# Softmax sums of layer 1: exponentials of two of four key tiles added by accumulating DMAs

## The chip, the cores and the metric

The kernel runs on one core of a Trainium2 chip. The metric is the time of the whole program on the device in microseconds (us), one launch, the median of several runs. The core has TensorE (PE: matrix products from SBUF into PSUM), VectorE (DVE), ScalarE (ACT), GpSimd (POOL) and SyncE (SP). Each works through its own queue of instructions in order, and semaphores tie the queues together. DMA engines, shared by all queues, move data between HBM and SBUF and inside SBUF.

## The reference

Input x is 8 sequences of 512 tokens and 256 channels, with a context of 512 x 128 for each. Layer 0 has self and cross attention and a quantized MLP; layer 1 has two attention blocks, each with an MLP behind it, and a feed-forward part with a convolution. The change lies in the attention of layer 1. It has 16 heads of width 32; `x` is the query side, and `y` is `x` itself in the first block ("a1") and the context in the second ("a2"):

```python
q = jnp.einsum('bsc,hcd->bhsd', xn, wq)
k = jnp.einsum('btc,hcd->bhtd', yn, wk)
v = jnp.einsum('btc,hcd->bhtd', yn, wv)
a = jax.nn.softmax(jnp.einsum('bhsd,bhtd->bhst', q, k) * D ** (-0.5), axis=-1)
if causal:
    mask = (jnp.arange(t)[None, :] > jnp.arange(s)[:, None]).astype(a.dtype)
    a = a * mask
o = jnp.einsum('bhst,bhtd->bhsd', a, v)
```

The mask of the first block comes after the softmax: the sum below the fraction runs over all 512 keys, and only the product with V leaves keys out. So every exponential goes into the sum, and the masked ones alone into the product.

## The kernel before

Everything here is float32 except the quantized products. The attention of layer 1 is cut into 16 slots (8 sequences x 2 blocks); a slot has 4 groups of 4 heads, a group has 4 key tiles of 128 keys. Layer 1 thus has 64 groups and 256 steps. In the causal block (`blk` 0, "strict") the key tiles are taken from the last to the first; in the other from the first to the last. "Third" and "fourth" tile below means `n` = 2 and `n` = 3 of that order, counted from 0.

A step has two halves in `steps1` (L2191 on). `front(g, n)` makes on TensorE the scores of one key tile for 4 heads into two PSUM tiles `ps_s`, and on ScalarE the exponentials into `pt`, 128 keys x 4 heads x 512 queries, 1 MB; there are three buffers of `pt` (`PTS`). In the causal block GpSimd cuts the diagonal part of `pt` out into `dg` (L2221). `back(g, n)` multiplies with V into the PSUM bank `ov`, of which there is one; the four tiles of a group add up in it.

The sums of the softmax: VectorE adds the exponentials of the first three tiles into `acc` (L2246 for the first two, L2248 for the third), and after the last tile TensorE multiplies a column of ones with `acc` and with the fourth `pt` into a PSUM bank `sm`, so that each of a head's 32 output rows holds the sum. VectorE then transposes, takes the reciprocal, transposes back (L2261 to L2264) and multiplies: `oT` = `ov` x `rb` (L2266). That reads `ov` in PSUM, so the bank comes free only then. `oT` (five buffers) goes into the MLP, `mlp1`, which asks for `q["oT", blk, g]`.

What runs in which order is written at build time by a planner. `weave_all` (L1824) holds a list of the attention steps and several chains of streams: `first` (end of layer 0), `pair1` (Q and K of a group), `mlp1` for each half of a sequence, `pre1`, `values2`, `last` (final feed-forward part) and others. A stream is a generator that yields `need(...)`: the tiles it waits for. The planner keeps a clock for every engine (`Pace`) and takes, of what can start within 0.3 us, that with the lowest place in the order. So every engine's order is fixed before the program runs, and an instruction that comes later than planned holds back all that stands behind it on its engine. At most two fronts run ahead of the backs. `front_at` and `back_at` say when a half may start; the last back of a group waits for `acc` and for a PSUM bank.

For a DMA the planner has this rule (`Pace.note`):

```python
if ins.opcode == "DMACopy":
    self.free[e] = t0 + 0.4
    ...
    self.wire = max(self.wire, t0 + 1.2) + n / 280e3
    end = self.wire + 1.2
```

`t0` is when the issuing engine is free and the sources are ready; `n` is bytes, 280e3 stands for 280 GB/s. Who wrote the destination before does not count for a DMA.

GpSimd has three kinds of work in this part: the selects into `dg`, the reciprocal roots of the layer norms (`mv`, L1975 to L1978, two short instructions for each), and additions of rows to residuals (L2040, L2043, L2144, L2146). GpSimd issues no DMA in layer 1 after its first loads. SP issues all others.

Of the kernel before, what the change touches and what calls it, by code (L numbers as in the profile page):

```python
# [15 lines left out]
P = 128  # L16
# [935 lines left out]
class Fast(General):  # L952
# [814 lines left out]
    def layer1_xattn(self):  # L1767
        nc, tc = self.nc, self.tc
        with (
            tc.tile_pool(name="w2", bufs=1) as wpool,  # L1770
            tc.tile_pool(name="wst", bufs=1) as self.wst,
            tc.tile_pool(name="work2", bufs=1) as work,
            tc.tile_pool(name="small2", bufs=1) as self.small,
            tc.tile_pool(name="st1", bufs=2, space=PSUM) as self.st,
            tc.tile_pool(name="ac1", bufs=1, space=PSUM) as self.ovp,
            tc.tile_pool(name="m1a", bufs=3, space=PSUM) as self.m1,
        ):
            self.work = work
            self.seqs = {b: {} for b in range(B)}

            self.hps = [wpool.tile([P, T // 2 + 3], F32, name=f"hp{i}") for i in range(2)]
            for t in self.hps:
                nc.gpsimd.memset(t, 0.0)
            self.wl = {}


            self.pairs = self.fronts = self.backs = self.zTs = self.nvt = 0
            self.li1s, self.mlps, self.loads, self.both_in = [0, 0], [0, 0], {}, {}

            self.rows = [(blk, bs) for bs in ROWS for blk in range(2)]  # L1790
            order = self.order = [(b, blk) for blk, bs in self.rows for b in bs]
            few, pairs, mlps, pres = [], [], [[], []], [[], []]

            for k, b in zip(FIRST_AT, range(B)):
                few.append(Stream(self.first(b), 3.8, 0.8, k, 1.0))
                if b == 1:
                    few.append(Stream(self.load_mlp(), 1.0, 1.0, k))
            for k, b in zip(LAST_AT, range(B - 1)):
                few.append(Stream(self.last(b), 10.5, 0.8, k, 1.0))
            few.sort(key=lambda s: s.base)  # L1800
            for k, (b, blk) in enumerate(order):
                for half in range(2):
                    mlps[half].append(Stream(self.mlp1(b, blk, half), 20.5, 0.88 if blk else 0.5, k + 1))
                    if not blk:
                        pres[half].append(Stream(self.pre1(b, half), 7.5, 0.65, k - 1, 2.0))
                for g in range(4):
                    pairs.append(Stream(self.pair1(b, blk, g), 3.0, 0.2, k + 0.25 * (g - 1)))
            for half in range(2):
                mlps[half][-1].base += 0.4 * half
                mlps[half].append(Stream(self.tail(half), 20.0, 1.0, 17 + 0.4 * half))  # L1810
            vals = [Stream(self.values2(b), 1.0) for b, blk in order if blk]
            self.final, self.tails = {}, [0, 0]
            diag = [Stream(self.diagonals(), 1.0, 0.1, 15.5)]
            self.keys_done, self.x0_read = False, 0
            keys = [Stream(self.keys2_rest(), 8.0 * (B - KEYS_FIRST), 1.0, -1.0)]
            self.weave_all(
                [self.steps1(b, blk) for b, blk in order], [few, pairs, *mlps, *pres, vals, diag, keys]
            )
            self.pace.close()

# [3 lines left out]
    def weave_all(self, attns, chains):  # L1824

        pace = self.pace
        steps = [(k + n / len(a), 1.0 / len(a), s) for k, a in enumerate(attns) for n, s in enumerate(a)]
        chains = [list(c) for c in chains]  # L1830

        def advance(c):
            s, w = c[0], pace.work
            s.need = next(s.gen, None)
            s.done += pace.work - w
            if s.need is None:
                c.pop(0)

        def starts(s):
            names, on_pe, _, on = s.need  # L1840
            t = max(pace.when(names), pace.free[on] - s.lag)
            return max(t, pace.place("m1")) if on_pe else t

        while self.backs < len(steps) or any(chains):
            now = pace.free.get("PE", 0.0)
            cands = []
            for c in chains:
                while c:
                    s = c[0]
                    if s.need is WAIT:  # L1850
                        advance(c)
                        if c and c[0] is s and s.need is WAIT:
                            break
                    elif not s.need[1] and starts(s) <= now:
                        advance(c)
                    else:
                        cands.append((s.base + s.share * s.done / s.total, starts(s), lambda c=c: advance(c)))
                        break
            if self.fronts < len(steps) and self.fronts - self.backs < 2:
                at, _, s = steps[self.fronts]  # L1860
                cands.append((at, s[0](), s[2]))
            if self.backs < self.fronts:
                at, d, s = steps[self.backs]
                cands.append((at + 1.05 * d, s[1](), s[3]))
            can = [c for c in cands if c[1] <= now + 0.3]
            pick = min(can, key=lambda c: c[0]) if can else min(cands, key=lambda c: (c[1], c[0]))
            assert pick[1] < 1e8
            pick[2]()
# [322 lines left out]
    def steps1(self, b, blk):  # L2191
# [6 lines left out]
        slot = self.slot_of(b, blk)  # L2198
        st = {}

        def front_at(g):
            if ("QK", blk, g) not in q or ("vt", blk) not in q:
                return 1e9
            return max(pace.when([Pace.name(t) for t in q["QK", blk, g]]), pace.place("st", 2))

        def front(g, n):
            kt = order[n]
            self.fronts += 1
            QT, KT = q["QK", blk, g]
            diag = slice(kt * P, (kt + 1) * P)  # L2210
            pss = [self.st.tile([P, 2, T], F32, tag="st", name="ps_s") for _ in range(2)][::-1]
            for j in (2, 3, 0, 1):
                r = slice(32 * j, 32 * j + 32)
                self.mm(pss[j // 2][:, j % 2, :], KT[r, diag], QT[r, :])
            pt = work.tile([P, 4, T], F32, tag="pt", name="pt", bufs=PTS)
            for jp in (1, 0):
                nc.scalar.activation(pt[:, 2 * jp : 2 * jp + 2, :], pss[jp], AF.Exp)  # L2217
            parts = [(pt, slice(0, T))]
            if strict:
                dg = work.tile([P, 4, P], F32, tag="dg", name="dg", bufs=2)  # L2220
                nc.gpsimd.affine_select(  # L2221
                    out=dg, in_=pt[:, :, diag], compare_op=ALU.is_gt, fill=0.0,
                    base=0, pattern=[[0, 4], [-1, P]], channel_multiplier=1,
                )
                parts = [(pt, slice(0, kt * P))] if kt else []
                parts.append((dg, diag))
            st[g, n] = (kt, pt, parts)

        def back(g, n):
# [11 lines left out]
                        n == 0 and i == 0, n == NT - 1 and i == len(parts) - 1,  # L2241
                    )

            if n == 1:
                st["acc"] = work.tile([P, 4, T], F32, tag="acc", name="acc")
                nc.vector.tensor_tensor(st["acc"], st["pt"], pt, ALU.add)  # L2246
            elif n == 2:
                nc.vector.tensor_tensor(st["acc"], st["acc"], pt, ALU.add)  # L2248
            st["pt"] = pt
            if n < NT - 1:  # L2250
                return
            sm = self.bank()
            for k, t in enumerate((st["acc"], pt)):
                for j in (2, 3, 0, 1):
                    self.mm(sm[32 * j : 32 * j + 32, :], self.ones, t[:, j, :], k == 0, k == 1)

            if g == 0:
                st["recs"] = work.tile([P, 4, 16], F32, tag="recs", name="recs", bufs=2)
# [3 lines left out]
            nc.vector.reciprocal(rec, rt[:, :, 0])  # L2262
            rb = work.tile([P, T], F32, tag="rt", name="rb", bufs=1)
            nc.vector.transpose(rb, rec.unsqueeze(2).to_broadcast([P, 16, 32]))  # L2264
            oT = q["oT", blk, g] = work.tile([P, T], F32, tag="oT", name="oT", bufs=5)
            nc.vector.tensor_tensor(oT, ov, rb, ALU.mult)  # L2266
            if g == 3:
                self.seen(st["recs"])

        def back_at(g, n):  # L2270
# [2 lines left out]
                return 1e9  # L2273
            _, pt, parts = st[g, n]
            t = pace.when([Pace.name(pt), Pace.name(q["vt", blk])] + [Pace.name(p) for p, _ in parts])
            if n == 0:
                return max(t, pace.place("ov1"))
            return max(t, pace.when([Pace.name(st["acc"])]), pace.place("m1")) if n == NT - 1 else t

        return [  # L2280
            (lambda g=g: front_at(g), lambda g=g, n=n: back_at(g, n),
             lambda g=g, n=n: front(g, n), lambda g=g, n=n: back(g, n))
            for g in range(4) for n in range(NT)
        ]
# [317 lines left out]
```

## Time and profile before

| | |
|---|---|
| median of 3 runs | 2784.82 us (2781.45 to 2786.3) |
| span of the profiled execution | 2779.7 us |
| mean granted TensorE clock | 0.959 |
| stage of the 64 groups, first to last product with ones | 938.4 to 2612.8 us |
| exponentials of one tile, two instructions of 128x1024 | 1.02 us each |
| select of a diagonal part, alone | 0.63 us |
| transposes of the sums, each | 0.71 us |
| multiplication `ov` x `rb` | 0.69 us |
| copy of 128x512 from PSUM to SBUF | 0.69 us on VectorE, 0.585 us on ScalarE |
| DMA engines, mean busy share in the stage | 0.17 |

The profile is of one execution. Busy time is the time in which an engine worked; the rest it waited or had nothing to do. Matrix products in float32 are two records each, so 8 records are 4 products. Where a line names a releaser ("<- DVE oT L2266"), the engine stood idle until that instruction was done. "ps" is any PSUM bank of the shared pool, "ps_s" the scores, "ov" the bank of the V product. A DMA's time to landing runs from its issue until its semaphore is complete.

### The profile page before, as it was taken

Reading aid. Unit: us, or ns where it says so; the run is one execution under the profiler, and the core shown is the slowest. Engines: PE = TensorE matmul, PEld = TensorE weight load, DVE = VectorE, ACT = ScalarE, POOL = GpSimd, SP = SyncE. Lnnn points to the kernel's source line nnn. Section 1 sums busy time; section 2 is a strip of 40 time slices with the busy share of each in tenths; the row PEclk is TensorE's granted clock in tenths of the full one; section 3 lists DMA queues with packets and bytes.
Section 4 is the critical chain, followed back from the end, with each engine's and each line's share of the span. In section 5 each row is a group of like instructions: output and inputs, shape, how many; then the busy total and the mean of one; then the engine's idle time right before and its main releaser. Section 6 shows DMA issues by size and latency. Waiting matters only on the chain.

```text
span 2779.7 us, 38478 instructions
## 1 busy us (share of the span) xinstructions
PE 2517.8 (91%) x15447; PEld 1223.8 (44%) x15452; DVE 1736.5 (62%) x3135; ACT 1452.2 (52%) x1803; POOL 614.8 (22%) x682
## 2 busy tenths in 40 slices
PE   7999999999786989999999999988999989999875
PEld 2333333333233344535554535545455454454554
DVE  4544554343476666564666777676777877767766
ACT  4666666656573554445444455444554555555421
POOL 2212222111001344231334231111114332101100
PEclk9999999999886999999999999999999999999987
DMA  3001120000364512211211013211021102211010
GB/s 113 25 27 50 50 73 16 20 31 12 118 261 173 178 46 99 80 46 42 76 60 63 16 54 107 69 38 58 24 82 60 43 4 89 71 45 43 23 38 17
DMA packets 76475, 176.55 MB, mean 64 GB/s; under 512 B 7424, under 2 KB 36480, under 8 KB 68992
## 3 DMA queue, kind: packets, MB, share of 16 engines
q1 hardware_dynamic: 73904, 170.81, 17.6%
q8 instruction: 123, 2.02, 0.3%
q0 software_dynamic: 800, 2.62, 0.3%
q10 hardware_dynamic: 1584, 0.58, 0.1%
q14 instruction: 64, 0.52, 0.1%
HBM read 111.07 MB, written 62.91 MB: 63 GB/s over the span
## 4 chain that ended last, share of the span: by engine, by line
PE 46%; DVE 13%; ACT 4%; POOL 2%; issue 2%; DMA 0%; ACTq 0%; POOLq 0%; DVEq 0%; SPq 0%
PE ps L1053 31%; PE ps_s L1053 8%; PE ov L1053 6%; ACT pt L2217 2%; PE ps L1056 1%; DVE hF L2332 1%; DVE acc L2246 1%; POOL dg L2221 1%; DVE rb L2264 1%; DVE hm L2342 1%; DVE z L144 1%; DVE mv L1971 1%; DVE rt L2261 1%; DVE oT L2266 1%; DVE acc L2248 1%
## 5 line engine op out<-in xcount | busy, mean ns | idle before, releaser
L2217 ACT ACTIVATE pt<-ps_s 128x1024 f32<-128x1024 f32 x512 | 496.3, 1021 | 418.0 <-PE ps_s L1053 313.6
L1053 PE MATMUL ps_s<-QT,KT 32*128 32x512 f32 (+3 forms) x4096 | 613.2, 607 | 28.3 <-ACT pt L2217 16.1
L1431 ACT ACTIVATE pt<-ps_s 128x1024 f32<-128x1024 f32 (+3 forms) x512 | 411.2, 862 | 202.6 <-PE ps_s L1053 194.3
L1053 PEld LDWEIGHTS ps_s<-QT,KT 32*128 32x128 f32 x4096 | 191.6, 184 | 368.0 <-issue 201.8
L1053 PE MATMUL ps<-x3T,li 128*128 128x256 f32 x1024 | 244.9, 391 | 3.9 <-DVE hp L2320 2.4
L1053 PE MATMUL ov<-pt,v 128*32 128x512 f32 (+3 forms) x2048 | 232.7, 525 | 13.5 <-POOL pt L1434 12.7
L1053 PE MATMUL ps<-li,hD 128*128 128x256 f32 x1024 | 239.1, 389 | 5.7 <-ACT hD L2164 5.7
L1053 PE MATMUL ov<-pt,vt 128*32 128x512 f32 (+3 forms) x1792 | 204.4, 526 | 36.2 <-DVE oT L2266 29.4
L1977 POOL TENSOR_SCALAR mv<-mv 128x2 f32<-128x2 f32 (+1 forms) x105 | 57.7, 550 | 770.4 <-DVE mv L1972 735.3
L2221 POOL TENSOR_SCALAR_AFFINE_SELECT dg<-pt 128x512 f32<-128x512 f32 x128 | 116.1, 908 | 505.6 <-ACT pt L2217 505.4
L1053 PEld LDWEIGHTS ps<-x3T,li 128*128 128x128 f32 x1024 | 192.5, 194 | 60.7 <-issue 18.4
L1053 PEld LDWEIGHTS ps<-li,hD 128*128 128x128 f32 x1024 | 193.8, 194 | 56.4 <-issue 14.5
L1434 POOL TENSOR_SCALAR_AFFINE_SELECT pt<-pt 128x512 f32<-128x512 f32 x128 | 86.3, 674 | 471.7 <-ACT pt L1431 470.0
L2248 DVE TENSOR_TENSOR acc<-acc,pt 128x2048 f32<-128x2048 f32 x64 | 149.4, 2334 | 4.3 <-ACT pt L2217 3.2
L2246 DVE TENSOR_TENSOR acc<-pt 128x2048 f32<-128x2048 f32 x64 | 149.2, 2332 | 1.1 <-ACT pt L2217 1.1
L1456 DVE STREAM_TRANSPOSE ot<-ov 128x512 f32<-128x512 f32 x64 | 45.8, 716 | 165.9 <-PE ov L1053 165.9
L2332 DVE SCALAR_TENSOR_TENSOR hF<-hp,cols,hF 128x256 f32<-128x256 f32 x224 | 114.6, 512 | 41.7 <-ACT hF L2323 35.6
L1053 PE MATMUL ps<-zT,a_wq 128*128 128x512 f32 x256 | 127.8, 623 | 2.1 <-DVE zT L2058 2.1
L1053 PE MATMUL ps<-li,oT 128*128 128x256 f32 x512 | 128.0, 394 | 1.7 <-DVE oT L2266 1.0
L1759 ACT ACTIVATE hD<-ps,cols 128x256 f32<-128x256 f32 x123 | 54.7, 471 | 137.1 <-PE ps L1053 100.5
L1053 PEld LDWEIGHTS ov<-pt,v 128*32 128x32 f32 x2048 | 40.4, 108 | 167.1 <-issue 100.2
L1053 PEld LDWEIGHTS ps<-li,oT 128*128 128x128 f32 x512 | 92.9, 191 | 47.7 <-issue 16.1
(305 smaller groups left out, 3654.9 us busy)
## 6 DMA issues: line engine op xcount, KB each, us to landing
hd<-h SPq DMA_DIRECT2D x16, 1024.0 KB, 3.9
hF<-hd SPq DMA_DIRECT2D x16, 1024.0 KB, 6.7
li<-in_w_a_dram SPq DMA_DIRECT2D x12, 1024.0 KB, 5.0
fw<-q_f_w SPq DMA_DIRECT2D x22, 512.0 KB, 5.5
xF<-xd SPq DMA_DIRECT2D x22, 512.0 KB, 5.1
kd<-k SPq DMA_DIRECT2D x8, 1024.0 KB, 3.9
vd<-v SPq DMA_DIRECT2D x8, 1024.0 KB, 5.2
res<-rd SPq DMA_DIRECT2D x32, 256.0 KB, 2.8
```

The lines of the kernel that those rows point to most:

```text
L144: self.nc.vector.tensor_scalar(out[:, i, :], x[:, i, :], mv[:, i, 0:1], rstd[:, i : i + 1], ALU.subtract, ALU.mult,)
L1053: self.nc.tensor.matmul(out, lhsT, rhs, start=start, stop=stop, skip_group_check=True)
L1431: nc.scalar.activation(pt[:, 2 * jp : 2 * jp + 2, lo:], pss[jp][:, :, lo:], AF.Exp)
L1434: nc.gpsimd.affine_select(out=diag, in_=diag, compare_op=ALU.is_ge, fill=0.0, base=0, pattern=[[0, 4], [1, P]], channel_multiplier=-1,)
L1456: nc.vector.transpose(ot.rearrange("p b d -> p (b d)"), ov)
L1759: self.nc.scalar.activation(out, ps, AF.Identity, bias=bias)
L1977: nc.gpsimd.tensor_scalar(rstd, mv[:, :, 1], EPS, None, ALU.add)
L2217: nc.scalar.activation(pt[:, 2 * jp : 2 * jp + 2, :], pss[jp], AF.Exp)
L2221: nc.gpsimd.affine_select(out=dg, in_=pt[:, :, diag], compare_op=ALU.is_gt, fill=0.0, base=0, pattern=[[0, 4], [-1, P]], channel_multiplier=1,
L2246: nc.vector.tensor_tensor(st["acc"], st["pt"], pt, ALU.add)
L2248: nc.vector.tensor_tensor(st["acc"], st["acc"], pt, ALU.add)
L2332: nc.vector.scalar_tensor_tensor(a, hp[:, half + k : half + k + n], self.col("conv_w", 3 * f + k), a, ALU.mult, ALU.add)
```

## The change

In the attention of layer 1 the exponentials of the first two tiles are still added by VectorE, now in the front of the third tile. Those of the third and the fourth are added to `acc` by two DMAs that GpSimd issues, `accum_op=ALU.add`, each from `pt` to `acc`, 1 MB. The product with ones then has `acc` alone as its input, four products a group instead of eight.

The V product is copied out of its bank into `oT` straight after its last part (`copy_of`, ScalarE or VectorE, whichever the planner finds free first). The rest of the group becomes a stream of its own, `end`, which waits for `acc`, makes the sums, and multiplies `oT` in place. `weave_all` takes the list `self.ends` as a further chain; streams are added to it as groups finish, so chains are no longer copied. As there is one buffer of `acc`, the front of a third tile may start only when the sums of the group before have been issued (`self.summed`). `back_at` for the last tile no longer waits for `acc` or for a bank.

```diff
@@ layer1_xattn
+            self.ends, self.summed = [], 0
...
             self.weave_all(
-                [self.steps1(b, blk) for b, blk in order], [few, pairs, *mlps, *pres, vals, diag, keys]
+                [self.steps1(b, blk) for b, blk in order], [few, pairs, *mlps, *pres, vals, diag, keys, self.ends]
             )
@@ weave_all
-        chains = [list(c) for c in chains]
@@ steps1
-        def front_at(g):
-            if ("QK", blk, g) not in q or ("vt", blk) not in q:
+        def front_at(g, n):
+            if n == 2 and self.summed < 4 * slot + g or ("QK", blk, g) not in q or ("vt", blk) not in q:
                 return 1e9
...
         def front(g, n):
             kt = order[n]
             self.fronts += 1
+            if n == 2:
+                acc = st["acc", g] = work.tile([P, 4, T], F32, tag="acc", name="acc")
+                nc.vector.tensor_tensor(acc, *st.pop("pts"), ALU.add)
...
             for jp in (1, 0):
                 nc.scalar.activation(pt[:, 2 * jp : 2 * jp + 2, :], pss[jp], AF.Exp)
+            if n < 2:
+                st["pts"] = st.get("pts", ()) + (pt,)
+            else:
+                nc.gpsimd.dma_start(st["acc", g], pt, accum_op=ALU.add)
...
-            if n == 1:
-                st["acc"] = work.tile([P, 4, T], F32, tag="acc", name="acc")
-                nc.vector.tensor_tensor(st["acc"], st["pt"], pt, ALU.add)
-            elif n == 2:
-                nc.vector.tensor_tensor(st["acc"], st["acc"], pt, ALU.add)
-            st["pt"] = pt
             if n < NT - 1:
                 return
+            oT = work.tile([P, T], F32, tag="oT", name="oT", bufs=5)
+            self.copy_of(oT, ov)
+            self.ends.append(Stream(end(g, st.pop(("acc", g)), oT), 1.0, 0.1, slot + 0.25 * g))
+
+        def end(g, acc, oT):
+            yield need(acc)
             sm = self.bank()
-            for k, t in enumerate((st["acc"], pt)):
-                for j in (2, 3, 0, 1):
-                    self.mm(sm[32 * j : 32 * j + 32, :], self.ones, t[:, j, :], k == 0, k == 1)
+            for j in (2, 3, 0, 1):
+                self.mm(sm[32 * j : 32 * j + 32, :], self.ones, acc[:, j, :])
+            self.summed += 1
...
-            oT = q["oT", blk, g] = work.tile([P, T], F32, tag="oT", name="oT", bufs=5)
-            nc.vector.tensor_tensor(oT, ov, rb, ALU.mult)
+            nc.vector.tensor_tensor(oT, oT, rb, ALU.mult)
+            q["oT", blk, g] = oT
...
-            if n == 0:
-                return max(t, pace.place("ov1"))
-            return max(t, pace.when([Pace.name(st["acc"])]), pace.place("m1")) if n == NT - 1 else t
+            return max(t, pace.place("ov1")) if n == 0 else t
```

More of the change, by code (lines that the diff above doesn't have):

```diff
@@ L2275, in back_at @@
             t = pace.when([Pace.name(pt), Pace.name(q["vt", blk])] + [Pace.name(p) for p, _ in parts])
-            if n == 0:
-                return max(t, pace.place("ov1"))
-            return max(t, pace.when([Pace.name(st["acc"])]), pace.place("m1")) if n == NT - 1 else t
+            return max(t, pace.place("ov1")) if n == 0 else t
         return [
-            (lambda g=g: front_at(g), lambda g=g, n=n: back_at(g, n),
+            (lambda g=g, n=n: front_at(g, n), lambda g=g, n=n: back_at(g, n),
              lambda g=g, n=n: front(g, n), lambda g=g, n=n: back(g, n))
```

## The prediction, made before the changed kernel ran

> **What bounds the kernel now.** I read the page first, then the stretch in which the change works, then TensorE's waits in that stretch, one group in order of time, and the transfers.
>
> From the page, busy time by engine, two of its costliest groups, and the chain by engine:
>
> ```profile
> PE 2517.8 (91%) x15447; PEld 1223.8 (44%) x15452; DVE 1736.5 (62%) x3135; ACT 1452.2 (52%) x1803; POOL 614.8 (22%) x682
> ...
> PE 46%; DVE 13%; ACT 4%; POOL 2%; issue 2%; DMA 0%; ACTq 0%; POOLq 0%; DVEq 0%; SPq 0%
> ...
> L2248 DVE TENSOR_TENSOR acc<-acc,pt 128x2048 f32<-128x2048 f32 x64 | 149.4, 2334 | 4.3 <-ACT pt L2217 3.2
> L2246 DVE TENSOR_TENSOR acc<-pt 128x2048 f32<-128x2048 f32 x64 | 149.2, 2332 | 1.1 <-ACT pt L2217 1.1
> ```
>
> TensorE is the bound, VectorE second. The 64 groups of layer 1 run from the first to the last product with ones, 938.4 to 2612.8 us. Busy time there:
>
> ```profile
> 938.40:2612.80 1674.40, 1565.40 (x9644) 820.62 (x9638) 1158.67 (x1987) 839.26 (x987) 437.71 (x442) 0.97 0.17 59
> ```
>
> The columns are TensorE, its weight loads, VectorE, ScalarE, GpSimd, clock, DMA share, GB/s. TensorE idles 1674.4 - 1565.4 = 109 us, VectorE is 69% busy. What TensorE waits for in that stretch (total, times, longest):
>
> ```profile
> PE ov L1053 <- DVE oT L2266: 29.4, 18, 4.9
> PE ps_s L1053 <- ACT pt L2217: 16.1, 25, 2.4
> PE ps L1056 <- DVE z L144: 14.9, 16, 3.0
> ...
> PE ov L1053 <- POOL dg L2221: 7.1, 10, 1.6
> PE ps L1053 <- DVE acc L2248: 4.7, 3, 2.3
> ```
>
> The reader is to see that VectorE's additions delay TensorE directly by only 4.7 us; the bank of the V product, held until the normalization, costs 29.4. One group's end, in order of time:
>
> ```profile
> 1504.19 1.04 PE L1053 MATMUL ps<-acc,ones 128*32 128x512 f32 x8
> ...
> 1505.05 1.04 PE L1053 MATMUL ps<-pt,ones 128*32 128x512 f32 x8
> ...
> 1506.02 1.14 PE L1053 MATMUL ps_s<-QT,KT 32*128 32x512 f32 x8
> ```
>
> From start to start the product with ones on `acc` holds TensorE 0.86 us, that on the fourth `pt` about as long. Transfers (KB each, us from issue to landing):
>
> ```profile
> hd<-h SPq DMA_DIRECT2D x16, 1024.0 KB, 3.9
> ...
> KT<-kd SPq DMA_DIRECT2D x32, 256.0 KB, 3.0
> ...
> xd<-xF SPq DMA_DIRECT2D x16, 256.0 KB, 2.1
> ...
> cT<-cd POOLq DMA_DIRECT2D x8, 256.0 KB, 4.3
> ```
>
> No transfer here goes from SBUF to SBUF and none accumulates: the dearest new operation has no row.
>
> **What the Trainium skill says.** "DMA: Bandwidth & Descriptors", section "Rules for kernel authors", says an accumulating DMA reads its destination and writes it later, so another write of the same bytes has to wait for its semaphore. The order of the changed program on GpSimd agrees: each second accumulation waits for the landing of the first. "Collectives: The Full Stack", section "The bandwidth ceiling: the fold count and why AG ≠ RS ≠ AR", says that a reducing transfer is slower than a copy because it reads two sources, not because of the addition. No transfer of the trace before shows that. "SBUF — State Buffer", section "Who interferes with whom", says a VectorE instruction with two SBUF inputs contends with a GpSimd one that reads SBUF. The trace agrees: at 1513.31 the select of L2221 beside the addition of 1512.40 took 1.84 us, alone 0.63.
>
> **What goes.** TensorE: one product with ones per group, 64 x 0.86 = 55 us, all on the bounding engine. VectorE: the addition of L2248, 149 us. Its direct price on TensorE is the 4.7 us above, the rest is slack for VectorE's other work. The wait of 29.4 us for the bank of `ov`: a copy that follows the last V product at once replaces a chain of sums, transpose, reciprocal, transpose and multiplication (1504.19 to 1508.63 in that group), so I count it as gone. GpSimd's selects lose half of the additions that they run into.
>
> **What comes.** The copies: in the changed order 31 are on VectorE (0.69 us each by its copies of L1325) and 33 on ScalarE (0.585 by L1323), 21 and 19 us on engines that are 69% and 50% busy; hidden behind TensorE, and if that cover were gone at most 0.6 us a group. The multiplication stays at about 0.69.
>
> The accumulations: 128 of 1 MB, two in a row for each group. What matters is L, from issue to landing. GpSimd's queue lands 256 KB in 4.3 us against SP's 3.0 for a load of the same size. The source is SBUF, not HBM: SP's stores of 256 KB take 2.1, about 0.9 less than loads. So 256 KB would be 3.4. The other 768 KB cost 3.9 - 2.1 = 1.8 us by the stores, 2.4 per MB. A copy is then 5.2; a second read of 1 MB adds 2.4: 7.6. I take 7.7, with 0.1 for the issue. Bounds: 5.2, if the second read is free, and 10.4, if everything is done twice. Not below 5.2, since a copy's bytes and the queue are both in rows of this trace.
>
> When must the sums be there? The planner prices a DMA by its own formula, 1.2 + 1.049 MB at 280 GB/s + 1.2 = 6.1 us, and starts it when the source is ready; it does not know that the second accumulation waits for the first. TensorE's order is fixed by that plan. I took the changed kernel's TensorE order and priced each instruction by its mean in the stage (scores of one tile 1.14 us, V product of a full tile 1.11, of a diagonal part 0.42, a 128x512 projection 0.98, a 128x256 step of the MLP 0.47 to 0.50, a transpose 0.18, bf16 0.125 or 0.21). Between the end of a group's fourth scores and its sums lie 12.0 us of such work (median of 64), from the third scores 16.4. An example, group 12: after its third scores come a V product 1.11, transposes 0.72, its fourth scores 1.14, a V product 1.11, a projection 1.96, the next group's first scores 1.14, transposes 0.72, a V product 1.11, the next group's second scores 1.14, V products and a bf16 block 1.11 + 2.00 + 1.11, then the sums: in all 14.4.
>
> Needed from the end of the third scores: 2.3 for the exponentials (two of 1.02 and the semaphore), L, L again. If the fourth exponential is later than the first landing, it counts instead. For group 12 that is 2.3 + 7.7 + 7.7 = 17.7 against 14.4, a stall of 3.3 us. In the causal half (32 groups) the fourth tile's select stands behind the second DMA on GpSimd's queue, so the last V product waits for 2.3 + L + 0.6 + 0.65; its median distance is 8.6. Summing the positive differences over the 64 groups:
>
> L 5.2: 40 us; 6.2: 72; 7.0: 118; 7.7: 168; 9.0: 270; 10.4: 410.
>
> At 7.7 the late select is 96 of the 168.
>
> **The sum.** My priced order holds 1569 us from the first scores to the last sums. The stage before is 1674.4. So 105 us go: 55 of products and about 50 of the 109 idle (29.4 for the bank, 4.7 for the addition, some 16 because waiting for a transfer lets VectorE and ScalarE catch up). Stalls at 7.7 bring 168. 2779.7 - 105 + 168 = 2843 us of span. The median of the runs is 5.1 above the profiled span, so 2848; a little for GpSimd being busy when the DMA could go (its `mv` pairs take 0.9 us, and those queued behind a waiting DMA delay VectorE's normalizations in turn) makes it 2850. What the new wait holds up on GpSimd's queue is the select, the `mv` pairs of the layer norms (whose z TensorE then transposes) and the additions to `res`; of the three buffers of `pt`, the one of the third tile is wanted again three score tiles later, at some 20 us (1674 / 64 = 26 us a group, four tiles), so I cost their longer life at nothing; with landings over 15 us the exponentials would wait for them.
>
> **Rivals.** (a) Faster: the landing is short, and what the products and the bank cost comes back. For it speaks that the DMA engines are busy 17% only and that the plan leaves 12 us after the fourth scores; against it, that two landings follow each other. It decides from L below 6.8, where the stalls equal 105. At L = 5.5 the stalls are 48: 2785 - 105 + 48 = 2728; with less of the idle absorbed, 2745. (b) Much slower: descriptors for accumulation are slow, or GpSimd is kept from writing them, L = 10.4 and more: 2785 - 105 + 410 = 3090; almost every group stalls. For it speaks that nothing in this trace shows such a transfer; against it, that the additions on VectorE are halved. (c) It does not do what it says: stalls merely displace idle time TensorE has already, no change, 2785. That needs L within 0.1 of 6.8.
>
> **Numbers.** Forecast (L 6.9 to 9.5): 0.55, its own range 2790 to 2990. (a) 0.25, (b) 0.16, (c) 0.04. What this measurement tells from no change is about 0.2%, 5.6 us. Faster 0.25, same 0.04, slower 0.71. The range 2745 to 3040 (L of 10: 2785 - 105 + 366 = 3046) leaves out somewhat under half of (a) and about two thirds of (b), 2 in 10 together.
>
> **What would show it.** Right: idle time of TensorE before the products with ones, or before the V product on the diagonal part, released by a DMA or by the select behind it, about 2.6 us a group; landing of the accumulations 7 to 8 us; VectorE's busy time down by some 130 us; TensorE's by 55; the wait for the bank of `ov` gone. Wrong: landing below 6.5 us and hardly a wait before the sums, or TensorE waiting elsewhere (on VectorE's `z`) more than on the sums. If the transfers land in 7 to 8 us and the time falls all the same, my distances along TensorE's order are too short, and that step is the one that failed.

## The result, and the profile after

The changed kernel takes 3095.25 us, median of 4 runs (3091.64 to 3100.83), against 2783.14 us (2781.26 to 2786.3) for the kernel before on the same chip. The ratio is 1.1123, 95% interval 1.1106 to 1.114: slower by 312 us. The forecast was 2850, range 2745 to 3040. The direction was right; the size was not, and the time lies outside the range.

The page of the kernel after. First line: busy time by engine. Second: the granted TensorE clock in 40 slices, in tenths. Then costly groups with busy time, mean ns, and the idle time ahead of them; last the new transfer with its median time to landing:

```profile
PE 2581.7 (83%) x14940; PEld 1242.4 (40%) x14940; DVE 1615.0 (52%) x3117; ACT 1483.4 (48%) x1830; POOL 651.8 (21%) x810
...
PEclk9999999998877889899998889999999899889977
...
L2224 POOL DMA_DIRECT2D acc<-pt x128 | 117.6, 918 | 1043.2 <-DMA acc<-pt 353.5
...
L1053 PE MATMUL ov<-dg,vt 128*32 128x128 f32 x1024 | 61.6, 318 | 161.6 <-POOL dg L2228 161.5
...
L1053 PE MATMUL ps<-acc,ones 128*32 128x512 f32 x512 | 81.2, 710 | 77.6 <-DMA acc<-pt 75.1
...
acc<-pt POOLq DMA_DIRECT2D x128, 1024.0 KB, 7.6
```

TensorE has four float32 products a group fewer, 512 records in all, yet its busy time rises from 2517.8 to 2581.7 us, and its share falls from 91% to 83%. Both can be true only if it waits longer and also runs slower while it works. The clock line shows the second. The landing takes 7.6 us in the middle; over all 128 the trace of the tile `acc` has:

```profile
DMA to landing us min/median/max: 6.9/7.6/12.9
```

Busy time in the stage of the 64 groups, first to last product with ones (columns as in the prediction: start:end, length, the five engines, clock, DMA share, GB/s):

```profile
954.60:2926.20 1971.60, 1619.65 (x9090) 835.07 (x9081) 1034.85 (x1962) 866.30 (x1013) 469.91 (x564) 0.90 0.48 116
```

The stage is 297 us longer (1971.6 against 1674.4) and starts 16 us later. TensorE's idle time in it goes from 109 to 352 us, its busy time from 1565.4 to 1619.7, its clock from 0.97 to 0.90. What it waits for in the stage (total, times, longest):

```profile
PE ov L1053 <- POOL dg L2228: 154.7, 47, 8.9
PE ps L1053 <- DMA acc<-pt: 75.1, 28, 7.8
PE ps_s L1053 <- ACT pt L2220: 26.6, 25, 3.4
PE ps_s L1053 <- ACT QT L2091: 18.2, 8, 6.2
```

The two places that the prediction named hold 230 us: the V product on the diagonal part (before: 7.1) and the product with ones (before: 4.7). The bank of `ov`, 29.4 before, is gone from the list. One group in order of time:

```profile
1513.23 1.94 ACT L2220 ACTIVATE pt<-ps_s 128x1024 f32<-128x1024 f32 x2 [0.38 <-PE ps_s L1053]
...
1515.47 0.94 POOL L2224 DMA_DIRECT2D acc<-pt  x1 [0.48 <-ACT pt L2220]
...
1517.06 1.94 ACT L2220 ACTIVATE pt<-ps_s 128x1024 f32<-128x1024 f32 x2 [1.88 <-issue]
...
1523.49 0.95 POOL L2224 DMA_DIRECT2D acc<-pt  x1 [5.30 <-ACT QT L2091]
1524.13 0.99 POOL L2228 TENSOR_SCALAR_AFFINE_SELECT dg<-pt 128x512 f32<-128x512 f32 x1
...
1525.17 0.43 PE L1053 MATMUL ov<-dg,vt 128*32 128x128 f32 x8 [2.77 <-POOL dg L2228]
...
1532.73 1.07 PE L1053 MATMUL ps<-acc,ones 128*32 128x512 f32 x8 [1.52 <-DMA acc<-pt]
```

The third tile's exponentials end at 1515.17 and their accumulation goes out at 1515.47. The fourth's end at 1519.00, but GpSimd issues the second accumulation only at 1523.49, 8.0 us after the first. (It names ScalarE's `QT` as the releaser because that ended last ahead of it. The DMA does not read `QT`, and the time from the first issue is one landing.) The select, an operation of 0.6 to 1.0 us whose input was ready at 1519.00, stands behind it on GpSimd's queue and starts at 1524.13. TensorE waits for it until 1525.17, and then, for the sums, until 1532.73 for the second landing.

What such a gap does to the clock is seen in short windows over the same group:

```profile
1517.00:1521.00 4.00, 4.00 (x42) 2.36 (x43) 1.49 (x3) 2.36 (x3) 1.02 (x3) 1.00 1.09 220
1521.00:1525.00 4.00, 1.40 (x4) 0.33 (x2) 0.00 (x0) 2.13 (x3) 1.51 (x3) 1.00 0.19 39
1525.00:1529.00 4.00, 3.83 (x28) 1.58 (x32) 1.38 (x2) 1.89 (x2) 1.95 (x3) 0.66 1.15 229
```

TensorE is busy at clock 1.00, then works 1.4 of 4 us, and in the next 4 us it is busy again but at 0.66. In that window 8 records of `ov<-pt,vt` with 384 columns take 1.51 us (from 1527.93); at 1509.14 the same took 0.85. The Trainium skill, "TensorE: Matmul & The Clock Gate", section "HAM oscillation — how this bites in real kernels", describes this: the clock is gated by recent activity, and idle gaps longer than about 3.4 us put TensorE back to half speed for a while. The trace agrees on the half speed: the clock record stands at 0.50 from 1526.25 to 1529.66 us, which is 3.41 us, and at 1.00 on both sides of it. In size it differs, for the gap here was 2.8 us only (the longest wait of the stage is 8.9).

### The profile page after: what moved, and what is told of

The parts are those of the page before. It is cut to its first block, busy times and chain, and to the rows that moved or that the text cites. A ratio compares the mean times of both kernels' runs of the same rounds, so it can differ in the third digit from the quotient of the medians.

```text
span 3094.4 us, 37779 instructions
## 1 busy us (share of the span) xinstructions
PE 2581.7 (83%) x14940; PEld 1242.4 (40%) x14940; DVE 1615.0 (52%) x3117; ACT 1483.4 (48%) x1830; POOL 651.8 (21%) x810
## 5 line engine op out<-in xcount | busy, mean ns | idle before, releaser
L1053 PE MATMUL ps_s<-QT,KT 32*128 32x512 f32 (+3 forms) x4096 | 640.7, 630 | 59.3 <-ACT pt L2220 26.6
L1053 PEld LDWEIGHTS ps_s<-QT,KT 32*128 32x128 f32 x4096 | 200.9, 190 | 398.5 <-issue 198.9
L2224 POOL DMA_DIRECT2D acc<-pt x128 | 117.6, 918 | 1043.2 <-DMA acc<-pt 353.5
L1053 PE MATMUL ps<-x3T,li 128*128 128x256 f32 x1024 | 256.1, 402 | 0.6 <-ACT x3T L2140 0.6
L1053 PEld LDWEIGHTS ps<-x3T,li 128*128 128x128 f32 x1024 | 199.0, 201 | 68.8 <-issue 23.3
L1053 PE MATMUL ov<-pt,vt 128*32 128x512 f32 (+3 forms) x1792 | 215.9, 545 | 6.8 <-ACT pt L2220 3.8
L1053 PE MATMUL ov<-dg,vt 128*32 128x128 f32 x1024 | 61.6, 318 | 161.6 <-POOL dg L2228 161.5
L1053 PE MATMUL ps<-acc,ones 128*32 128x512 f32 x512 | 81.2, 710 | 77.6 <-DMA acc<-pt 75.1
L1053 PE MATMUL ps<-li,oT 128*128 128x256 f32 x512 | 137.4, 416 | 0.1
L1761 DVE TENSOR_SCALAR hD<-ps,cols 128x256 f32<-128x256 f32 x137 | 62.9, 480 | 112.7 <-PE ps L1053 84.7
```

The source lines that it names most:

```text
L1053: self.nc.tensor.matmul(out, lhsT, rhs, start=start, stop=stop, skip_group_check=True)
L1761: self.nc.vector.tensor_scalar(out, ps, bias, None, ALU.add)
L2224: nc.gpsimd.dma_start(st["acc", g], pt, accum_op=ALU.add)
```

## The experiments

The theories, in the words used below. Landing (A, in its parts): the chain of two accumulations comes too late, at the sums and, through GpSimd's queue, at the select. Traffic (B): 134 MB more through the DMA engines slow the others down. Split (C): what was rearranged for the DMAs costs time without any DMA. Later it was divided into the copies out of the bank (D), the sums as a stream of their own (E), and the first addition in another place (F). All ratios are to runs of the kernel before on the same chip. One caution holds for every step below: each edit makes the planner write another order for all engines, and how far the time moves with such a change of order alone was not measured. A step of 10 or 20 us can't be put down to its edit with certainty.

**VectorE in place of both DMAs.** In the back of the third and fourth tile VectorE adds; one product with ones remains. So that the weights of the last feed-forward part are loaded before the final part uses them, the planner holds that part back until then.

```diff
-            else:
-                nc.gpsimd.dma_start(st["acc", g], pt, accum_op=ALU.add)
...
+            if n >= 2:
+                nc.vector.tensor_tensor(st["acc", g], st["acc", g], pt, ALU.add)
```

> As the changed kernel, with each accumulating DMA replaced by an addition on VectorE: three additions a group there, one product with ones. Theories A and B: TensorE has 55 us less to do than before, VectorE some 150 us more (busy 80% of the stage instead of 69%), so VectorE is late more often: 2720 to 2800. Theory C: 2900 or more.

Measured: 2907.58 us, ratio 1.0449 (1.0429 to 1.0468). Its stage:

```profile
942.50:2713.30 1770.80, 1573.30 (x9088) 815.38 (x9087) 1274.62 (x2014) 894.33 (x1077) 454.71 (x441) 0.95 0.16 55
```

Without any DMA the kernel is still 122 us slower than before, in the range of theory C. VectorE is 72% busy, TensorE idles 198 us. Some 22 of the 122 us lie behind the stage (188 us of the profiled execution against 167 before), where the final part was held back; what the holding back costs was not tried alone. So the DMAs were not all of it, and the addition of the fourth tile on VectorE is no cheap way to save the product either.

**The select first.** The changed kernel with the select issued ahead of the accumulation of the same tile.

```diff
-            if n < 2:
-                st["pts"] = st.get("pts", ()) + (pt,)
-            else:
-                nc.gpsimd.dma_start(st["acc", g], pt, accum_op=ALU.add)
             parts = [(pt, slice(0, T))]
             if strict:
...
                 parts.append((dg, diag))
+            if n < 2:
+                st["pts"] = st.get("pts", ()) + (pt,)
+            else:
+                nc.gpsimd.dma_start(st["acc", g], pt, accum_op=ALU.add)
```

> Only the order on GpSimd changes: the select of the diagonal part is issued ahead of the accumulating DMA of the same tile. Theory A (waits: the second accumulation holds GpSimd's queue until the first has landed, TensorE stops for the select and for the sums, and in these stops loses clock): the 155 us of waiting for the select in the stage fall below 40, part of it comes back as waiting for the sums, TensorE's clock rises from 0.90 to about 0.93, time 2900 to 2990. Theory B (traffic: the 137 MB moved beside the products slow TensorE): the clock stays at 0.90, time 2960 to 3000. Theory C (the split into a later stream costs): 3050 or more.

Measured: 3011.87 us, ratio 1.0817 (1.0799 to 1.0835), 83 us less than after. Waits in its stage:

```profile
PE ps L1053 <- DMA acc<-pt: 100.7, 34, 8.3
PE ov L1053 <- POOL dg L2224: 34.5, 21, 5.4
```

Of the 154.7 at the select 34.5 are left, but 25.6 of the gain come back at the sums: GpSimd still waits 336.9 us with its accumulations for an earlier one (353.5 after). The clock of the stage rises to 0.91 only, not to 0.93, and the time lies between what theories B and C expected, above A.

**The third tile alone by DMA.** The fourth goes back to its own product with ones, eight products a group; all else as after.

```diff
-            else:
+            elif n == 2:
                 nc.gpsimd.dma_start(st["acc", g], pt, accum_op=ALU.add)
...
-            for j in (2, 3, 0, 1):
-                self.mm(sm[32 * j : 32 * j + 32, :], self.ones, acc[:, j, :])
+            for k, t in enumerate((acc, pt)):
+                for j in (2, 3, 0, 1):
+                    self.mm(sm[32 * j : 32 * j + 32, :], self.ones, t[:, j, :], k == 0, k == 1)
```

> The third tile is still added by a DMA, the fourth by a second product with ones, as in the kernel before: one accumulation a group, none waits for another. Theory A: no wait of GpSimd for a landing, hardly a wait before the sums, clock back to 0.96, time 2740 to 2800. Theory B: half the traffic, so about half of the lost clock stays (0.93), time 2830 to 2900. Theory C: still over 2900.

Measured: 2849.37 us, ratio 1.0235 (1.0217 to 1.0252). Waits in its stage:

```profile
PE ov L1053 <- POOL dg L2228: 24.0, 17, 4.5
PE ps_s L1053 <- ACT QT L2091: 23.4, 11, 3.9
PE ps L1053 <- DMA acc<-pt: 22.7, 12, 5.0
```

The second accumulation in place of the second product costs 246 us of the 312. It is not the transfer as such: 64 of them are still there, landing in 7.2 us (median). The clock of the stage is back at 0.97, as theory A said, but the time is not: it lies in B's range, which the next experiment explains without traffic.

**The split without any DMA.** VectorE adds the first two tiles in the front and the third in the back, the fourth has its own product; copy out of the bank and stream `end` as after.

```diff
-                nc.gpsimd.dma_start(st["acc", g], pt, accum_op=ALU.add)
...
+            if n == 2:
+                nc.vector.tensor_tensor(st["acc", g], st["acc", g], pt, ALU.add)
...
-        def end(g, acc, oT):
-            yield need(acc)
+        def end(g, acc, pt, oT):
+            yield need(acc, pt)
```

> No DMA: VectorE adds the first three tiles and the fourth has its own product with ones, as in the kernel before; the copy out of the bank, the later normalization and the stream of its own stay. Theories A and B: 2740 to 2785, the wait of 29 us for the bank gone. Theory C: 2900 or more.

Measured: 2841.76 us, ratio 1.0203 (1.0186 to 1.0221). Waits in its stage:

```profile
PE ps_s L1053 <- ACT pt L2220: 30.3, 31, 3.3
PE ov L1053 <- POOL dg L2226: 21.8, 13, 6.4
PE ps_s L1053 <- ACT QT L2091: 18.5, 11, 2.8
PE ps_s L1053 <- ACT KT L1759: 13.2, 14, 3.5
```

The wait for the bank is gone, and the kernel is 57 us slower than before: scores now wait for ScalarE (16.1 for `pt` before). The time lies between the two expectations: the split costs, but less than theory C wanted. The third tile's accumulation by DMA (the experiment above, 8 us more than this one) is almost neutral here.

**Copies on VectorE alone**, in the split kernel:

```diff
-            self.copy_of(oT, ov)
+            nc.vector.tensor_copy(oT, ov)
```

> The split alone (no DMA, as in e4, 2842 us), with every copy out of the bank on VectorE. In e4 ScalarE stood 52 us before its copies, waiting for the last V product with exponentials and Q behind them. Theory D (the copy holds up ScalarE's queue): those waits go, TensorE waits less for exponentials, Q and K, time 2785 to 2815. Theory E (the planner simply writes a worse order once the sums are a stream of their own): 2830 to 2860.

Measured: 2831.10 us, ratio 1.0164 (1.0145 to 1.0184): 11 us less by the ratios than with the planner's choice between ScalarE and VectorE. That is in the range of theory E; the choice of the engine is a minor part.

**The copy alone, in line.** The kernel before, with the copy ahead of the sums and the multiplication in place:

```diff
+            oT = q["oT", blk, g] = work.tile([P, T], F32, tag="oT", name="oT", bufs=5)
+            self.copy_of(oT, ov)
             sm = self.bank()
...
-            nc.vector.tensor_tensor(oT, ov, rb, ALU.mult)
+            nc.vector.tensor_tensor(oT, oT, rb, ALU.mult)
```

> The kernel before with the copy out of the bank added, and the sums, reciprocal and multiplication left where they were, directly after the last V product: no stream of its own. Theory D: the copy costs here too, 2800 to 2840. Theory E: no loss, and the wait of 29 us for the bank goes: 2755 to 2790.

Measured: 2791.38 us, ratio 1.0027 (1.0017 to 1.0036). The largest waits in its stage:

```profile
PE ps L1056 <- DVE z L144: 20.9, 14, 2.9
PE ps_s L1053 <- ACT KT L1759: 11.9, 9, 3.1
```

The bank's 29.4 us are no longer among them, but TensorE's idle time in the stage is 110 us, as before the change (109). The wait moved to others, and the kernel loses 8 us instead of gaining 29, just above the range of theory E.

**The planner told of the landing.** The changed kernel; the planner's rule for DMAs into `acc` now lets each wait for what wrote `acc` last and prices it 7.8 us, and 0.9 us of GpSimd. They also no longer take their turn with other transfers in the planner's `wire`.

```diff
-        if ins.opcode == "DMACopy":
+        if ins.opcode == "DMACopy" and out.startswith("acc"):
+            t0 = max(t0, self.done[out] + self.SIGNAL)
+            self.free[e] = t0 + 0.9
+            end = t0 + 7.8
+        elif ins.opcode == "DMACopy":
             self.free[e] = t0 + 0.4
```

> The changed kernel; only the planner's rule for the accumulating DMAs is another: they start when the one before has landed, take 7.8 us and GpSimd 0.9 us. Theory A1 (half of the loss or more comes from an order that was fixed for transfers of 6.1 us beside each other): TensorE's waits for the select and for the sums (230 us in the stage) fall below 100, clock 0.94 or more, time 2880 to 2960. Theory A2 (two landings in a row take too long for one accumulator, whatever the order): the waits move into other places, time 3030 to 3120.

Measured: 2928.27 us, ratio 1.0529 (1.0498 to 1.056). Waits in its stage:

```profile
PE ov L1057 <- POOL dg L2232: 60.5, 39, 6.6
PE ps_s L1057 <- ACT pt L2224: 51.1, 41, 4.6
PE ps L1057 <- DMA acc<-pt: 33.6, 18, 5.6
```

The same DMAs with nearly the same landing (7.4 us), in an order made with about their true time, are 167 us cheaper, as theory A1 expected. The two places fall from 230 to 94 us, the clock of the stage rises from 0.90 to 0.94.

**The traffic alone.** The kernel before, and SP writes the `pt` of each third and fourth tile to HBM, 128 writes of 1 MB, for which no computation waits but the next use of the buffer.

```diff
+            if n >= 2:
+                nc.sync.dma_start(self.dump[(self.fronts // 2) % 4], pt.rearrange("p j t -> p (j t)"))
```

> The kernel before with 128 extra transfers that nobody waits for: SP writes the third and fourth pt of each group, 1 MB each, to a scratch place in HBM. Theory B (the traffic slows TensorE): the clock falls below 0.94 and the time rises by 80 us or more. Theory A: the clock stays at 0.95 to 0.96, time 2780 to 2820, the rise being loads that stand behind a write on SP's queue.

Measured: 2797.95 us, ratio 1.0046 (1.0029 to 1.0063). Its stage:

```profile
937.80:2627.20 1689.40, 1574.16 (x9642) 823.04 (x9634) 1145.23 (x1971) 851.46 (x1006) 432.93 (x442) 0.97 0.37 137
```

At 137 GB/s, more than the 116 of after, the clock stays at 0.97 and the kernel loses 14 us. Traffic of this size explains neither the 312 us nor the clock. (These transfers write to HBM, not to SBUF; accumulating traffic that nobody waits for was not tried.)

**Both repairs.** The planner told and the select first, the two edits above together:

```diff
-        if ins.opcode == "DMACopy":
+        if ins.opcode == "DMACopy" and out.startswith("acc"):
+            t0 = max(t0, self.done[out] + self.SIGNAL)
...
                 parts.append((dg, diag))
+            if n < 2:
+                st["pts"] = st.get("pts", ()) + (pt,)
+            else:
+                nc.gpsimd.dma_start(st["acc", g], pt, accum_op=ALU.add)
```

> Both cures at once: the planner knows that accumulations follow each other and take 7.8 us (e8, 2928 us), and the select is issued ahead of the DMA (e2). Theory A1 (GpSimd's queue and the fixed order explain what the second accumulation costs beyond the split, 2842 us in e4): 2850 to 2890. Theory A2 (the chain of two landings on one accumulator costs by itself): 2905 to 2935, as e8.

Measured: 2914.81 us, ratio 1.0459 (1.0443 to 1.0475): 180 us less than after, 65 more than with one accumulation, and in the range of theory A2, not A1. On GpSimd, over the whole run, and at TensorE in the stage:

```profile
L2237 POOL DMA_DIRECT2D acc<-pt x128 | 115.1, 899 | 789.7 <-DMA acc<-pt 323.8
```

```profile
PE ps_s L1057 <- ACT pt L2224: 54.4, 54, 4.1
PE ps L1057 <- DMA acc<-pt: 53.6, 18, 7.6
PE ov L1057 <- POOL dg L2228: 24.7, 13, 6.0
```

GpSimd still stands 324 us at its accumulations until an earlier one has landed. Neither of the two orders tried on its queue removes that wait: one puts the same tile's select behind it, the other still the next group's.

**The end in line.** The split kernel without DMAs, its sums again straight after the last V product, which waits again for `acc` and for a bank; copy and moved first addition are kept.

```diff
-            self.ends.append(Stream(end(g, st.pop(("acc", g)), pt, oT), 1.0, 0.1, slot + 0.25 * g))
+            for _ in end(g, st.pop(("acc", g)), pt, oT):
+                pass
...
-            return max(t, pace.place("ov1")) if n == 0 else t
+            if n == 0:
+                return max(t, pace.place("ov1"))
+            return max(t, pace.when([Pace.name(st["acc", g])]), pace.place("m1")) if n == NT - 1 else t
```

> The split of e4 (2842 us; no DMA), with the sums, reciprocal and multiplication issued directly after the last V product instead of by a stream of its own; the first addition stays in the front of the third tile, as in e4. Theory E (the stream of its own makes the planner's order worse): about e7, 2780 to 2805. Theory F (the place of the first addition and the gate on the third front make it worse): about e4, 2825 to 2850.

Measured: 2765.02 us, ratio 0.9919 (0.9904 to 0.9934): the fastest kernel here, 77 us less than the split with the stream. Its stage:

```profile
938.90:2597.50 1658.60, 1563.79 (x9644) 823.93 (x9635) 1173.79 (x2004) 869.60 (x1035) 439.31 (x442) 0.98 0.18 59
```

The time is below both expectations, nearer to E's. So neither the copy nor the moved addition was the loss.

**One accumulation in line.** The kernel before, only its third tile's addition a DMA, the planner told as above.

```diff
-                nc.vector.tensor_tensor(st["acc"], st["acc"], pt, ALU.add)
+                nc.gpsimd.dma_start(st["acc"], pt, accum_op=ALU.add)
```

> The kernel before with one edit: the third tile is added to acc by an accumulating DMA instead of VectorE, issued after the tile's last V product, so no select stands behind it; the planner is told 7.8 us. Everything else in line, as before. Theory A: one landing a group is hidden, VectorE has 149 us less to do, 2755 to 2790. If the landing is late at the sums: 2790 to 2840.

Measured: 2899.91 us, ratio 1.0424 (1.0404 to 1.0445), above both expectations. Waits in its stage:

```profile
PE ps L1057 <- DMA acc<-pt: 62.3, 22, 9.9
PE ov L1057 <- DVE oT L2270: 37.4, 26, 4.1
```

In this arrangement a single landing is late at the sums, even with its time in the plan: the DMA goes out in the back of the third tile, not in its front, and the sums follow in line. With the front and the stream, and without the planner told, the same 64 accumulations gave 2849 us; which of these makes the difference was not tried.

**The stream with the old condition.** Where the 77 us between the stream and the line come from:

```diff
-            return max(t, pace.place("ov1")) if n == 0 else t
+            if n == 0:
+                return max(t, pace.place("ov1"))
+            return max(t, pace.when([Pace.name(st["acc", g])]), pace.place("m1")) if n == NT - 1 else t
```

> e4_split_alone with one edit: the last back of a group waits again, as before the change, for acc and for a bank of the pool; the sums stay a stream of their own. It stands between e4 (2842 us, stream, no such wait) and e11 (2765, in line, with the wait). If it was the missing wait that put the products with ones in the wrong place of TensorE's order (the planner lets the V product go early and fills the gap with scores of the next group), the time is 2765 to 2785. If it is the stream as such (its queue, the condition on the third front), it stays at 2825 to 2845. In between: both take part.

Measured: 2796.36 us, ratio 1.0043 (1.0033 to 1.0053): in between. The missing condition on the last V product is 45 of the 77 us, the stream itself some 31. In the programs' order on TensorE the number of score tiles of the next group ahead of the sums tells the same: before the change and in line it is one for 62 of 64 groups, with this condition 1 for 37 and 2 for 25, without it 0 for 19, 1 for 16 and 2 for 29. Why a group with its sums between other scores costs more was not taken further.

## Why the prediction was right in direction and wrong in size

The runs split the 312 us along a path of single steps: copy and moved addition -21 us, the sums as a stream without the old condition +77, the third tile by DMA +8, the fourth by a second, chained DMA in place of a product +246, together 310 between medians of different chips. Telling the planner the DMA's time takes 167 off the changed kernel, the select's place 13 more, and 65 remain against the kernel with one accumulation, whose planner was not told. Such shares depend on the order of the edits: without the planner told, the select's place alone gave 83. What the 65 consist of stays open.

By the prediction's own terms, in the spans of the profiled executions: forecast 2843, measured 3094.4, a difference of 251 us. Its sum expected 227 us of idle TensorE time in the stage (109 - 50 + 168). One slip in it is apart from all terms: the 1569 us of the priced order run from the first scores, the 1674.4 of the stage before from the first sums, which come 17 us later (921.4 and 938.4 us in the trace before). Over the same stretch the working saves 122 us and not 105, so the forecast stood 17 us nearer to the result than its own working.

| term | predicted | measured | miss |
|---|---|---|---|
| stalls at select and sums | 168 | 230 | +62 |
| other idle time of TensorE in the stage (59 = 109 - 50) | 59 | 122 | +63 |
| TensorE's work in the stage, less 55 of products | 1510 | 1620 | +109 |
| start of the stage | unchanged | 16 later | +16 |

*Landing.* Predicted 7.7 us between bounds of 5.2 and 10.4, measured 7.6 in the middle. As a sum the estimate from the stores, the queue and a second read held; no run shows its parts one by one. So rival (b), which named 3090 us, was near the time by another cause than the one it gave: it wanted a landing of 10.4.

*Stalls.* The place was right, the sum was 62 us short: 154.7 against 96 at the select, 75.1 against 72 at the sums. The agreement at the sums is in part luck: with the select ahead, where TensorE is stopped less before, they hold it 100.7 us. The step that was mis-sized is the late select: it was priced as 2.3 + L + 0.6 + 0.65 with GpSimd otherwise free and the first accumulation issued at once. In the trace the first accumulation goes out 1.7 us after the end of the third exponentials and the second 8.4 us after the first (medians of the 64 groups), where the prediction had about 0.3 and 7.7. GpSimd waits 353.5 us in all at the accumulations for earlier ones, and selects and additions to `resP` queue behind. The remark about GpSimd being busy gave that 2 us.

*"About 50 of the 109 idle" go.* This step failed. The bank's wait did go, but nothing of the idle time with it: in the kernel with the copy alone it stays at 110, and with the moved addition too, in line, it is 95. And the stream, costed at nothing, took more than that back: the split without DMAs is 57 us slower than before, and its idle time is 129. That waiting for a transfer lets VectorE and ScalarE catch up was argued from nothing measured.

*A term was missing: the clock.* This step failed too, and it is the largest miss. TensorE's work was summed at durations of the stage before, at clock 0.97, and an increase of idle time was taken to cost its own length. The stage ran at 0.90, and its work took 109 us more than predicted; the product with ones took 710 ns against 603. The runs put the clock with the idle time and not with the traffic:

| kernel | idle TensorE in the stage, us | at half speed in the stage, us | clock in the stage | time, us |
|---|---|---|---|---|
| end in line | 95 | 82 | 0.98 | 2765 |
| stream with the old condition | 107 | 96 | 0.97 | 2796 |
| before | 109 | 85 | 0.97 | 2783 |
| copy alone, in line | 110 | 89 | 0.97 | 2791 |
| before, 134 MB written to HBM | 115 | 109 | 0.97 | 2798 |
| split, no DMA | 129 | 123 | 0.96 | 2842 |
| split, copies on VectorE | 130 | 99 | 0.97 | 2831 |
| third tile by DMA | 144 | 99 | 0.97 | 2849 |
| VectorE in place of both DMAs | 198 | 188 | 0.95 | 2908 |
| one accumulation in line | 207 | 154 | 0.96 | 2900 |
| planner told, select first | 211 | 240 | 0.93 | 2915 |
| planner told | 211 | 219 | 0.94 | 2928 |
| select first | 274 | 331 | 0.91 | 3012 |
| after | 352 | 393 | 0.90 | 3095 |

No run changes the gaps alone. But the clock records of the 14 traces show what goes ahead of each fall. They hold two values only, 1.00 and 0.50, and every spell between two changes is a whole multiple of 3.41 us. Divided on that grid, the stretches at full speed in the 14 stages give windows of 3.41 us. In 229 of them TensorE worked less than 40% of the time, and half speed followed on all 229. In 5415 it worked 80% or more, and half speed followed on none; in between, on 151 of 880. The window ahead of the fall at 1526.25 has 1.08 us of work. In the stage after, 308 us more than before ran at half speed; an estimate from that, with TensorE busy throughout, is 154 us of lost work at most, and 109 were measured.

This is no matter of the new transfers. In the seven kernels without any added transfer the counts are 73 of 73 and 0 of 2806, in the six with accumulations 148 of 148 and 0 of 2205. It also says why the order of the table by idle time isn't strict: idle time costs clock where it leaves such a window, and much less where it is spread in short waits.

*The rest.* One product a group did go from TensorE, 55 us by the starts before; but in neither pair that differs by it (after and the third tile by DMA, VectorE in place of the DMAs and the split) was the kernel with one product the faster. VectorE's busy time fell by 121.5 us (130 predicted). The longer life of `pt` was costed at nothing, and that held in the main. ScalarE's exponentials waited for whatever adds to or reads `acc` (us, times), first before, then after, then after for the accumulating DMAs alone:

```profile
  ACT pt L2217: 56.1, 28
  ACT pt L2220: 45.2, 24
  ACT pt L2220: 12.1, 6
```

The start of the stage, 16 us later, was not in the sum: the first sums have two landings ahead of them (with one accumulation the stage starts at 941.9, with two at 954.6). The selects gained next to nothing from fewer additions beside them: 890 ns in the mean against 908.

## What to carry to other kernels

When work goes from an engine to DMAs that add to the same buffer, count the landings in a row, and everything that stands behind the second issue on its queue; and if the order is written at build time, give the planner the landing before judging the change (167 of 312 us here). Idle time of TensorE should be priced above its own length where it leaves a window of 3.41 us mostly empty, since the clock falls to half after it: here 243 us more of idle time came with 109 us more of work. A wait that a copy removes is worth something only if no other wait stands right behind it, and moving the end of a group to a stream of its own changes the order of everything: try each of these alone.

## What the runs showed of the hardware that was not expected

- TensorE's clock went to half for 3.41 us or a multiple of it after every window of 3.41 us, on the grid of the clock record, in which it worked less than 40% at full speed (229 of 229), and never after one in which it worked 80% or more (0 of 5415). A gap of 2.8 us was enough. Over the stage the clock fell from 0.97 to 0.90 with the idle share from 6.5% to 17.9%.
- 128 writes of 1 MB from SBUF to HBM beside a TensorE that is over 90% busy cost 14 us in all, at a clock of 0.97 with and without them; a write landed in 4.3 us (median), an accumulation of the same size from SBUF to SBUF in 7.6, and the issue of one held GpSimd 0.92 us.
- Some other transfers land later beside the accumulations: `hF<-hd`, 1 MB, in 9.2 us against 6.7, `xF<-xd`, 512 KB, in 7.2 against 5.1; `xP<-xd`, 256 KB, stays at 5.0.
